# Layer 0 of a four-layer network: six of a Mamba item's 24 products with B formed with tokens on partitions by ScalarE and turned back by TensorE

## The chip, the core and the metric

The kernel is one program on one core of a Trainium2 chip. The metric is the device time in microseconds of the whole program, which computes four layers; only layer 0 is touched. The engines are TensorE (PE in the profile; its weight loads are PEld), VectorE (DVE), ScalarE (ACT), GpSimd (POOL) and SyncE (SP), which here issues every DMA. Each engine carries out its own instructions in the order in which they were put in its queue. SBUF is the on-chip memory, PSUM the small one into which TensorE writes.

## The reference

Layer 0 is two Mamba blocks one after the other, then a mix with a pooled branch and a batch normalisation. Cut to what matters:

```python
B, C, H, W = (4, 96, 64, 64)            # L = 4096 tokens
NLAYERS, DSTATE, EXPAND, DCONV = (2, 16, 2, 4)   # DIN = 192
...
    xz = h @ in_w
    xs, z = jnp.split(xz, 2, axis=-1)
    ...
    xc = jax.nn.silu(xc)
    dbl = xc @ xproj_w
    dt = dbl[..., :DTRANK]
    Bm = dbl[..., DTRANK:DTRANK + DSTATE]
    Cm = dbl[..., DTRANK + DSTATE:]
    delta = jax.nn.softplus(dt @ dt_w + dt_b)
    A = -jnp.exp(A_log)
    dA = jnp.exp(delta[..., None] * A)
    dBx = delta[..., None] * Bm[:, :, None, :] * xc[..., None]
    ...
    hstates = jax.lax.associative_scan(comb, (dA, dBx), axis=1)[1]
    y = jnp.einsum('blds,bls->bld', hstates, Cm) + Dp * xc
    y = y * jax.nn.silu(z)
    return y @ out_w
```

So for each of 192 channels and 16 states, along 4096 tokens: a factor `dA`, a term `dBx` (delta times xc times B), a running sum of the two, and a product with C that is summed over the states.

## The kernel before

**Items and tiles.** The work is cut into 32 items: 4 chunks of 1024 tokens, 2 blocks, 4 batch elements (`items`). An item has 192 x 16 = 3072 recurrences, which are 24 tiles of 128 partitions by 1024 tokens (`order`). A tile (p, g, j) has 4 states (group g of four) by 32 channels (half j of third p). A tile needs four steps:

- `exp` (ACT, line 464): dA = exp(A x delta). `ddb`, delta with each channel repeated for four states, comes by DMA from a copy in DRAM.
- the product of `udb` (delta times xc, repeated in the same way) with B. For eight tiles of an item, `pool_tiles`, POOL does it (`times_b`, line 470, output `up`) with `brep`, B repeated over 32 channels, which comes by DMA. For the other 16, PE repeats B into the PSUM tile `rep` (`rep`, line 450) and DVE multiplies (line 482).
- `scan` (DVE, line 486): the recurrence, output `hs`.
- `times_c` (POOL, line 492): `hs` times `crep`, C repeated.

PE then adds up the states of `hs` (`sum_y`, line 511) into `y`, to which `start_y` has put Dp x xc. Three times an item DVE multiplies `y` with silu(z) (`gate`), then `project` and `finish` form the block's output.

**First stage.** `first_stage(k)` makes what item k needs, spread over the two items before it: the normalisation (`center`, `nt`, `n`), `xc` (16 matmuls for each of three parts, line 210), its Silu, `dbl` (dt, B and C), `delta` with its Softplus, `z` with its Silu, `du` = delta x xc (three parts on POOL, line 378), and the DMAs that write `dd`, `ud` and `cd` to DRAM and load them repeated. Each step has a slot, `at_slot(t)`: it is put in the queues at tile t of the item before. Silu and Softplus need another table of ScalarE than Exp; `exp_set()` loads the Exp table back after each.

**Order.** The order is written out by hand: the loop over m at the end of the layer goes through all 768 tiles, and each pass issues the scan of tile m, then `rep` or `exp` of tile m + 1, `exp` of tile m + 3 (unless that is a POOL tile), `times_c` of m - 1, `keep_state` of m - 3, `times_b` as `b_slots` says, `sum_y`, `gate`, `project` and `finish`, and last the first-stage steps of that slot. POOL's and DVE's instructions, as all others, stand in this order.

**PSUM.** Its eight banks are full: two for `ps` (first stage and projection), two for `x` (one tile `rep`), two for `u` (one tile: the products `u` and, for POOL tiles, the exps `dap`), two for `y`.

```python
            eight = [(0, 0), (0, 1), (3, 0), (1, 1), (1, 0), (3, 1), (2, 0), (2, 1)]
            order = [(p, g, j) for p in range(3) for g, j in eight]
            pool_tiles = (2, 5, 7, 10, 13, 15, 18, 21)
            group_starts = (0, 3, 6, 8, 11, 14, 16, 19, 22)
```

Of the kernel before, what the change touches and what calls it, by code (L numbers as in the profile page):

```python
# [50 lines left out]
class Net:  # L51
# [43 lines left out]
    def layer0(self, dram, scratch):  # L95
        tc, nc, ins = self.tc, self.nc, self.ins
        x_in = ins["x"]
        with ExitStack() as ctx:
# [3 lines left out]
            psum_y = ctx.enter_context(tc.tile_pool(name="l0y", bufs=2, space=PSUM))  # L102
# [23 lines left out]
            sel_b = load(cp, "sel_b", [64, 4, 128])  # L126
# [24 lines left out]
            AHEAD = 3  # L151

# [48 lines left out]


            both = [(at, slice(64 * q, 64 * q + 64)) for q, at in enumerate(halves)]

            def spread(ws, rhs, p):

                ps = tile_ps(128)
                for k, (w, shift) in enumerate(ws):
                    for at, rows in both:
                        nc.tensor.matmul(  # L210
                            ps[rows],
                            w[:, 64 * p : 64 * p + 64],
                            rhs[:, at.start + shift : at.stop + shift],
                            start=k == 0,
                            stop=k == len(ws) - 1,
                            skip_group_check=True,
                        )
                return ps
# [10 lines left out]
            def global_pool():  # L229

                for b in range(B):
                    for s in range(NSC):
                        xt = wk.tile([128, T + 1], F32, name="gp_x", tag="hs", bufs=9)[:C, :T]
# [21 lines left out]
            def first_stage(k):  # L255
# [29 lines left out]
                def _():  # L285
                    m["nt"] = cp.tile([128, 8, C], F32, name="nt", tag="nt")
# [51 lines left out]
                @at_slot(4)  # L338
                def _():
                    nc.scalar.activation(m["xc"], m["xc"], AF.Silu)  # L340
                    exp_set()

# [3 lines left out]
                @at_slot(7)  # L346
# [4 lines left out]
                @at_slot(8)  # L351
# [6 lines left out]
                parts_of("delta", [(dtw[:, i], 0)], dbl, ((9, 10), (9, 10), (10, 11)), 1)  # L358

                @at_slot(11)  # L360
# [4 lines left out]
                parts_of("z", [(w_z[:, i], 3)], n, ((11, 12), (12, 13), (13, 14)), 3)  # L365

                @at_slot(12)
# [5 lines left out]
                def du(p):  # L373
# [3 lines left out]
                    u = wk.tile([128, 1, MB], F32, name="du", tag="du")  # L377
                    nc.gpsimd.tensor_mul(u, m["delta"][:, of], m["xc"][:, of])  # L378
# [3 lines left out]

                for p in range(3):
                    at_slot(14 + 3 * p)(lambda p=p: du(p))

                @at_slot(16)
                def _():
                    nc.scalar.activation(m["z"], m["z"], AF.Silu)
                    exp_set()


# [4 lines left out]
                for g, t in ((0, 10), (1, 21), (3, 23), (2, 25)):  # L396
                    at_slot(t)(lambda g=g: load_c(m, g))
                at_slot(19)(lambda: load_b(m, 3))
                at_slot(15)(lambda: load_b(m, 2))
                return steps  # L400

# [9 lines left out]
            def load_c(made, g):  # L411
                made["crep", g] = load_s(made, "crep", NST + 4 * g, 5)

            def load_b(made, g):
                made["brep", g] = load_s(made, f"brep{g}", 4 * g, 1)
# [20 lines left out]
            def on_pool(m):  # L436
                return m % NTL in pool_tiles
# [16 lines left out]

            def exp(m):
# [10 lines left out]
            def times_b(m):  # L466
# [3 lines left out]
                nc.gpsimd.tensor_mul(u, made[k]["ud", h, j], made[k]["brep", g])  # L470

            def scan(m, x):
# [4 lines left out]
                if on_pool(m):  # L477
                    u = made[k].pop(("u", t))
                else:

                    u = x if on_pool(m + 1) else psum_x.tile([128, T], F32, name="u", tag="u")
                    nc.vector.tensor_mul(u, made[k]["ud", h, j], x)  # L482
                hs = made[k]["hs", t] = wk.tile([128, T + 1], F32, name="hs", tag="hs", bufs=9)
# [71 lines left out]
            b_slots = {2: 5, 4: 7, 7: 10, 9: 13, 12: 15, 15: 18, 18: 21, 23: NTL + 2}  # L555
# [3 lines left out]
            for m in sorted(stages[0])[:4]:  # L559
                for f in stages[0].pop(m):  # L560
                    f()
            prepare()
            wk = ctx.enter_context(tc.tile_pool(name="l0w", bufs=1))
            with tc.manual_schedule(engines=engines):
                gp = global_pool()
                first = min(stages[0])
                for m in range(first, last + 19):
# [3 lines left out]
                    if 0 <= m + 1 < last:  # L571
                        if on_pool(m + 1):
                            exp(m + 1)
                        elif (t + 1) % NTL in group_starts:
# [7 lines left out]
                    if -1 <= m and t in b_slots and m - t + b_slots[t] < last:  # L582
# [767 lines left out]
def _constants():  # L1350
# [3 lines left out]
    sel_b = np.stack([(k[:64, None] % 32 == 4 * g + p[None] // 32) for g in range(4)], 1)  # L1354
# [127 lines left out]
```

## Time and profile before

| | |
|---|---|
| median of three runs | 3918.07 us (3902.56 to 3920.63) |
| the profiled execution | 3925.66 us, its span 3923.9 us |
| granted TensorE clock, mean over the span | 0.855 |
| first and last scan of layer 0 | start at 77.3 us, end at 2612.5 us |
| DMA | 463.31 MB, 46.7% of 16 engines |

The span is what the profile covers, from the first instruction to the last. In the page, a group of instructions gives the line, the engine, the operation, output<-inputs by the program's names, the shapes and the count; after the bar stand the busy time of all and the mean in nanoseconds of one, then the idle time of the engine just before them and what ended most of it. In a timeline the columns are start, duration, engine, line, operation, tiles, count, and in brackets the idle time before and what ended it. In an answer on waits they are who waited for whom, the sum, how often and the longest. An engine's idle time counts only where others wait for that engine.

### The profile page before, as it was taken

The numbers are of one execution on the slowest core, as the hardware profiler recorded it, in microseconds if no ns is written. First come the engines' busy times: TensorE is split into PE (matmuls) and PEld (weight loads), VectorE is DVE, ScalarE is ACT, GpSimd is POOL, SyncE is SP. The second block draws the span as 40 slices with busy tenths as digits, with TensorE's granted clock in tenths as the row PEclk, the third lists the DMA queues.
The fourth block names the chain that finished last, engine by engine and source line by source line (L and its number), as shares of the span: only waits on it lengthen the run. The fifth ranks groups of instructions, "written<-read, shape, count | busy, mean of one in ns | idle before, by whom it ended". The sixth has DMA issues, their size and how long they took to land. (4 is left out here: it accounts for less than half of the span.)

```text
span 3923.9 us, 43975 instructions
## 1 busy us (share of the span) xinstructions
PE 3205.9 (82%) x13534; PEld 1294.8 (33%) x13534; DVE 3154.4 (80%) x2772; ACT 2420.6 (62%) x4644; POOL 2911.4 (74%) x1443
## 2 busy tenths in 40 slices
PE   6887878877878788877878887755899988899988
PEld 3222222222222222222222222115644534666643
DVE  5999999999999999999999999973374385444649
ACT  4666667766766676666766666532254676666557
POOL 2999999999999999999999999961101064444427
PEclk7788878898788888888878878766899999999989
DMA  7567656675666566756676566636300000011101
GB/s 188 135 162 171 151 130 168 164 170 131 164 158 173 132 165 154 172 140 158 153 171 150 143 161 163 159 90 211 140 1 0 1 1 6 15 36 33 39 7 59
DMA packets 179828, 463.31 MB, mean 118 GB/s; under 512 B 52852, under 2 KB 54782, under 8 KB 176256
## 3 DMA queue, kind: packets, MB, share of 16 engines
q1 hardware_dynamic: 179592, 460.49, 46.7%
q8 instruction: 108, 1.77, 0.2%
q14 instruction: 128, 1.05, 0.1%
HBM read 386.81 MB, written 73.50 MB: 117 GB/s over the span
## 5 line engine op out<-in xcount | busy, mean ns | idle before, releaser
L492 POOL TENSOR_TENSOR hs<-hs,crep 128x1024 f32<-128x1024 f32 x768 | 1797.7, 2364 | 48.0 <-DVE hs L486 26.1
L450 PE MATMUL rep<-dbl,sel_b 32*128 32x512 f32 x1152 | 407.8, 785 | 495.8 <-DVE hs L486 428.3
L464 ACT ACTIVATE da<-ddb,nega 128x1024 f32<-128x1024 f32 x512 | 584.9, 1150 | 47.2 <-DVE hs L486 40.0
L470 POOL TENSOR_TENSOR up<-udb,brep 128x1024 f32<-128x1024 f32 x256 | 605.2, 2364 | 8.8 <-DMA brep<-cd 8.8
L464 ACT ACTIVATE dap<-ddb,nega 128x1024 f32<-128x1024 f32 x256 | 286.0, 1117 | 409.3 <-DVE hs L486 408.5
L511 PE MATMUL y<-hs,sel_r 128*32 128x512 f32 x3072 | 476.4, 690 | 5.5 <-POOL hs L492 5.5
L486 DVE TENSOR_TENSOR_SCAN hs<-da,state,rep 128x1024 f32<-128x1024 f32 x192 | 450.8, 2348 | 16.7
L486 DVE TENSOR_TENSOR_SCAN hs<-da,state,u 128x1024 f32<-128x1024 f32 x192 | 450.9, 2348 | 11.2 <-DVE u L482 1.4
L486 DVE TENSOR_TENSOR_SCAN hs<-dap,state,up 128x1024 f32<-128x1024 f32 x192 | 446.7, 2326 | 0.4 <-ACT dap L464 0.4
L210 PE MATMUL ps<-n,w_x 97*64 97x512 f32 x1536 | 408.0, 679 | 9.3 <-ACT n L319 6.6
L482 DVE TENSOR_TENSOR u<-udb,rep 128x1024 f32<-128x1024 f32 x256 | 314.7, 1229 | 74.4 <-PE rep L450 46.0
L450 PEld LDWEIGHTS rep<-dbl,sel_b 32*128 32x128 f32 x1152 | 107.0, 214 | 794.5 <-issue 595.7
L482 DVE TENSOR_TENSOR rep<-udb,rep 128x1024 f32<-128x1024 f32 x256 | 310.3, 1212 | 0.2
L1040 POOL CAST hq<-y 128x1536 fp8e5<-128x1536 f16 x64 | 94.0, 1469 | 219.3 <-issue 122.6
L210 PEld LDWEIGHTS ps<-n,w_x 97*64 97x64 f32 x1536 | 118.6, 153 | 295.2 <-issue 243.5
L511 PEld LDWEIGHTS y<-hs,sel_r 128*32 128x32 f32 x3072 | 65.2, 114 | 336.5 <-issue 208.5
L378 POOL TENSOR_TENSOR du<-delta,xc 128x512 f32<-128x512 f32 x96 | 122.6, 1277 | 64.7 <-ACT delta L362 50.2
L914 POOL MEMSET h<- 1x4096 f32 x1 | 3.5, 3507 | 212.8 <-DVE n L820 212.8
L1179 POOL TENSOR_TENSOR av<-av,ec 128x780 f32<-128x780 f32 x32 | 58.8, 1837 | 133.2 <-ACT av L1176 133.2
L486 DVE TENSOR_TENSOR_SCAN hs<-da,rep 128x1024 f32<-128x1024 f32 x64 | 146.5, 2289 | 5.4
L224 PE MATMUL ps<-xc,xproj 64*102 64x512 f32 x384 | 147.3, 924 | 3.5 <-ACT xc L340 3.5
L486 DVE TENSOR_TENSOR_SCAN hs<-da,u 128x1024 f32<-128x1024 f32 x64 | 146.4, 2288 | 3.7 <-DVE u L482 0.5
(262 smaller groups left out, 6137.7 us busy)
## 6 DMA issues: line engine op xcount, KB each, us to landing
ddb<-dd SPq DMA_DIRECT2D x768, 128.0 KB
udb<-ud SPq DMA_DIRECT2D x768, 128.0 KB
crep<-cd SPq DMA_DIRECT2D x512, 128.0 KB
brep<-cd SPq DMA_DIRECT2D x256, 128.0 KB
dd<-delta SPq DMA_DIRECT2D x64, 384.0 KB
ud<-du SPq DMA_DIRECT2D x192, 128.0 KB
band<-in_band SPq DMA_DIRECT2D x24, 1024.0 KB
x<-in_x SPq DMA_DIRECT2D x32, 384.0 KB
```

The source lines that it names most:

```text
L210: nc.tensor.matmul(ps[rows], w[:, 64 * p : 64 * p + 64], rhs[:, at.start + shift : at.stop + shift], start=k == 0, stop=k == len(ws) - 1, ...
L224: nc.tensor.matmul(ps, w[rows, p], x[rows, p], start=start and p == 0, stop=p == 2)
L378: nc.gpsimd.tensor_mul(u, m["delta"][:, of], m["xc"][:, of])
L450: nc.tensor.matmul(x[:, at], sel_b[rows, order[t][1]], made[k]["dbl"][rows, at], start=True, stop=True)
L464: nc.scalar.activation(da, made[k]["dd", h, j], AF.Exp, scale=nega[:, col : col + 1])
L470: nc.gpsimd.tensor_mul(u, made[k]["ud", h, j], made[k]["brep", g])
L482: nc.vector.tensor_mul(u, made[k]["ud", h, j], x)
L486: nc.vector.tensor_tensor_scan(hs[:, 1:], made[k].pop(("da", t)), u, 0.0 if s == 0 else st, ALU.mult, ALU.add)
L492: nc.gpsimd.tensor_mul(hs[:, :T], hs[:, 1:], made[k]["crep", order[t][1]])
L511: nc.tensor.matmul(made[k]["y", p][row : row + 32], sel_r, made[k]["hs", t][:, at], start=False, stop=True, skip_group_check=True,)
L1040: nc.gpsimd.tensor_copy(q, y2, saturate=False)
L1179: nc.gpsimd.tensor_add(v[:, 2:4], v[:, 0:2], ec)
```

## The change

An item's 24 products with B are split differently: 12 on DVE (groups g = 0 and 1), 6 on POOL (`GP` = 3), and 6 (`GA` = 2) with tokens on partitions. For these, PE turns `du` (`turn_du`: 12 transposes of 128 x 128) and B (8 small ones) so that tokens lie on partitions, ACT copies them out (`keep_du`, `bt`) and multiplies (`weigh`: 32 instructions of 192 elements each, B as the scalar of each partition), and PE turns the results back (`turn_u`: 8 transposes of 128 x 128 a tile) into the PSUM tile `x`, from which the scan reads.

With it: the order of the tiles is new (in p = 0 four tiles of DVE, then turned, POOL, turned, POOL; the others alike), `b_slots` with it; `du` of p = 1 goes to DVE; the first stage's slots move; the Silu of `z` stands beside that of the next item's `xc`; `y` has one PSUM buffer in place of two, and the freed bank takes the new turns and `z` (`turn_ps`); `hs` has 8 buffers in place of 9, `nt` lies in the buffers of `up`, `crep` has one buffer for each of four names in place of five in rotation, and B is loaded for one group in place of two; every product of DVE writes `u`, where before half of them were written over `rep`; `sum_y`, `gate`, `project` and `finish` move by one to four slots.

```diff
-            psum_y = ctx.enter_context(tc.tile_pool(name="l0y", bufs=2, space=PSUM))
+            psum_y = ctx.enter_context(tc.tile_pool(name="l0y", bufs=1, space=PSUM))
...
+            def turn_ps():
+                return psum_y.tile([128, MB], F32, name="t_ps", tag="t")
...
-                    m["nt"] = cp.tile([128, 8, C], F32, name="nt", tag="nt")
+                    if k:
+                        nt = wk.tile([128, T], F32, name="nt", tag="up", bufs=2)
+                    else:
+                        nt = first_pool.tile([128, T], F32, name="nt")
+                    m["nt"] = nt[:, : 8 * C].rearrange("p (q c) -> p q c", q=8)
...
                     nc.scalar.activation(m["xc"], m["xc"], AF.Silu)
+                    if k:
+                        silu_z(k - 1)
                     exp_set()
+
+                if k == len(items) - 1:
+                    at_slot(28)(lambda: (silu_z(k), exp_set()))
 
                 nb = 6 * NST + DTR
                 dbl = m["dbl"] = dbls[k % 2]
 
-                @at_slot(7)
+                @at_slot(6)
                 def _():
                     m["ps"] = [tile_ps(128), tile_ps(128)]
                     join([ps[:nb] for ps in m["ps"]], xproj[:, :, i], m["xc"])
 
-                @at_slot(8)
+                @at_slot(7)
                 def _():
                     for at, ps in zip(halves, m["ps"]):
                         nc.scalar.copy(dbl[:nb, at], ps[:nb])
                     cd = m["cd"] = dram.tile([2 * NST, T], F32, name="cd", tag="cd", bufs=2)
                     nc.sync.dma_start(cd, dbl[: 2 * NST])
 
-                parts_of("delta", [(dtw[:, i], 0)], dbl, ((9, 10), (9, 10), (10, 11)), 1)
-
-                @at_slot(11)
+                @at_slot(8)
+                def _():
+                    m["tb"] = turn_ps()[:, : 8 * 2 * NST].rearrange("p (q s) -> p q s", q=8)
+                    for q in range(8):
+                        nc.tensor.transpose(
+                            m["tb"][:, q], dbl[: 2 * NST, q * 128 : q * 128 + 128], self.ident[: 2 * NST, : 2 * NST]
+                        )
+
+                parts_of("delta", [(dtw[:, i], 0)], dbl, ((8, 9), (8, 9), (9, 10)), 1)
+
+                @at_slot(9)
+                def _():
+                    m["bt"] = cp.tile([128, 8, 4], F32, name="bt", tag="bt")
+                    nc.scalar.copy(m["bt"], m["tb"][:, :, 4 * GA : 4 * GA + 4])
+
+                @at_slot(10)
                 def _():
                     nc.scalar.activation(m["delta"], m["delta"], AF.Softplus)
                     exp_set()
 
-                parts_of("z", [(w_z[:, i], 3)], n, ((11, 12), (12, 13), (13, 14)), 3)
-
-                @at_slot(12)
+                @at_slot(11)
...
-                    u = wk.tile([128, 1, MB], F32, name="du", tag="du")
-                    nc.gpsimd.tensor_mul(u, m["delta"][:, of], m["xc"][:, of])
+                    u = m["du"] = wk.tile([128, 1, MB], F32, name="du", tag="du")
+                    (nc.vector if p == 1 else nc.gpsimd).tensor_mul(u, m["delta"][:, of], m["xc"][:, of])
                     to = m["ud"].rearrange("(p c) t -> c p t", p=3)[:, of]
                     for at, rows in both:
                         nc.sync.dma_start(to[:, :, at], u[rows])
 
+                def turn_du(p):
+                    ps = m["ut", p] = turn_ps() if p == 0 else tile_ps(128)
+                    for q in range(4):
+                        at = slice(q * 128, q * 128 + 128)
+                        nc.tensor.transpose(ps[:, at], m["du"][:, 0, at], self.ident)
+
+                def keep_du(p):
+                    if p == 0:
+                        udt = wk.tile([128, 3, MB], F32, name="udt", tag="delta", bufs=1)
+                        m["udt"] = udt.rearrange("p a b -> p (a b)").rearrange("p (q d) -> p q d", q=8)
+                    nc.scalar.copy(
+                        m["udt"][:, :, 64 * p : 64 * p + 64].rearrange("t (h q) d -> t q h d", h=2),
+                        m.pop(("ut", p)).rearrange("t (q h d) -> t q h d", q=4, h=2),
+                    )
+
                 for p in range(3):
-                    at_slot(14 + 3 * p)(lambda p=p: du(p))
-
-                @at_slot(16)
-                def _():
-                    nc.scalar.activation(m["z"], m["z"], AF.Silu)
-                    exp_set()
-
+                    at_slot(12 + 2 * p)(lambda p=p: turn_du(p))
+                    at_slot(11 + 2 * p)(lambda p=p: du(p))
+                    at_slot((16, 16, 17)[p])(lambda p=p: keep_du(p))
+
+                def weigh(of):
+                    if of[0] == 0:
+                        m["uta"] = wk.tile([128, 8, 6, 128], F32, name="uta", tag="uta", bufs=1)
+                    for e in of:
+                        q, s4 = divmod(e, 4)
+                        nc.scalar.mul(
+                            m["uta"][:, q, :, 32 * s4 : 32 * s4 + 32],
+                            m["udt"][:, q].rearrange("t (c d) -> t c d", d=32),
+                            m["bt"][:, q, s4 : s4 + 1],
+                        )
+
+                for e in range(9):
+                    at_slot(18 + e)(lambda e=e: weigh(range(32 * e // 9, 32 * (e + 1) // 9)))
+
+                def into_z(p):
+                    if p == 0:
+                        m["z"] = wk.tile([128, 3, MB], F32, name="z", tag="z", bufs=2)
+                    nc.scalar.copy(m["z"][:, p], m.pop(("z", p)))
+
+                for p in range(3):
+                    at_slot(20 + p)(lambda p=p: into_z(p))
+                    at_slot(19 + p)(lambda p=p: m.update({("z", p): spread([(w_z[:, i], 3)], n, p, turn_ps())}))
...
-                for g, t in ((0, 10), (1, 21), (3, 23), (2, 25)):
-                    at_slot(t)(lambda g=g: load_c(m, g))
-                at_slot(19)(lambda: load_b(m, 3))
-                at_slot(15)(lambda: load_b(m, 2))
+                for g, t in ((0, 22), (1, 23), (GA, 25), (GP, 27)):
+                    at_slot(t)(lambda g=g: load_c(m, g, k))
+                at_slot(17)(lambda: load_b(m))
                 return steps
+
+            def silu_z(k):
+                nc.scalar.activation(made[k]["z"], made[k]["z"], AF.Silu)
...
-                made["crep", g] = load_s(made, "crep", NST + 4 * g, 5)
-
-            def load_b(made, g):
-                made["brep", g] = load_s(made, f"brep{g}", 4 * g, 1)
+            def load_c(made, g, k):
+                made["crep", g] = load_s(made, f"crep{(g + 2 * k) % 4}", NST + 4 * g, 1)
+
+            def load_b(made):
+                made["brep"] = load_s(made, "brep", 4 * GP, 1)
...
-            eight = [(0, 0), (0, 1), (3, 0), (1, 1), (1, 0), (3, 1), (2, 0), (2, 1)]
-            order = [(p, g, j) for p in range(3) for g, j in eight]
-            pool_tiles = (2, 5, 7, 10, 13, 15, 18, 21)
-            group_starts = (0, 3, 6, 8, 11, 14, 16, 19, 22)
+            dd, ap = [(g, j) for g in range(2) for j in range(2)], [(GA, 0), (GP, 1), (GA, 1), (GP, 0)]
+            order = [(p, g, j) for p, gs in enumerate((dd + ap, dd[:2] + ap + dd[2:], ap + dd)) for g, j in gs]
...
+            def turned(m):
+                return order[m % NTL][1] == GA
...
+            def turn_u(m):
+
+                k, t = divmod(m, NTL)
+                p, g, j = order[t]
+                x = psum_x.tile([128, T], F32, name="ua", tag="x")
+                for q in range(8):
+                    nc.tensor.transpose(x[:, q * 128 : q * 128 + 128], made[k]["uta"][:, q, 2 * p + j], self.ident)
...
+                elif turned(m):
+                    u = x
                 else:
 
-                    u = x if on_pool(m + 1) else psum_x.tile([128, T], F32, name="u", tag="u")
+                    u = psum_x.tile([128, T], F32, name="u", tag="u")
                     nc.vector.tensor_mul(u, made[k]["ud", h, j], x)
-                hs = made[k]["hs", t] = wk.tile([128, T + 1], F32, name="hs", tag="hs", bufs=9)
+                hs = made[k]["hs", t] = wk.tile([128, T + 1], F32, name="hs", tag="hs", bufs=8)
...
-            b_slots = {2: 5, 4: 7, 7: 10, 9: 13, 12: 15, 15: 18, 18: 21, 23: NTL + 2}
+            b_slots = {8: 11, 9: 13, 14: 17, 15: 19, 21: NTL + 5, 1: 7}
...
+                        elif turned(m + 1):
+                            x = turn_u(m + 1)
+                        elif order[(t + 1) % NTL][2] == 0:
                             x = rep(m + 1)
...
-                            if at == 8 * p + 3:
+                            if at == 8 * p + 5:
                                 start_y(k0, p)
 
-                            if at - 8 * p in (4, 6, 8, 10):
-                                sum_y(k0, at - 4)
-                            if at == 8 * p + 11:
+                            if at - 8 * p in (5, 7, 9, 11):
+                                sum_y(k0, at - 5)
+                            if at == 8 * p + 12:
                                 gate(k0, p)
-                        if at == 34:
+                        if at == 31:
                             made[k0]["x"] = load_x(*items[k0])
-                        if at == 39:
+                        if at == 35:
                             project(k0)
-                        if at == 41:
+                        if at == 37:
```

More of the change, by code (lines that the diff above doesn't have):

```diff
@@ L125, in layer0 @@
             sel_r = load(cp, "sel_r", [128, 32])
-            sel_b = load(cp, "sel_b", [64, 4, 128])
+            sel_b = load(cp, "sel_b", [64, 2, 128])
             xproj = load(cp, "xproj", [128, 3, 2, 3 * 2 * NST + DTR])
@@ L151, in layer0 @@
             AHEAD = 3
+            GA, GP = 2, 3
             def prepare():
@@ L200, in tile_ps, with spread @@
                 return psum.tile([128, MB], F32, name="ps", tag="ps")[:rows]
+            def turn_ps():
+                return psum_y.tile([128, MB], F32, name="t_ps", tag="t")
             both = [(at, slice(64 * q, 64 * q + 64)) for q, at in enumerate(halves)]
-            def spread(ws, rhs, p):
-                ps = tile_ps(128)
+            def spread(ws, rhs, p, ps=None):
+                if ps is None:
+                    ps = tile_ps(128)
                 for k, (w, shift) in enumerate(ws):
@@ L232, in global_pool @@
                     for s in range(NSC):
-                        xt = wk.tile([128, T + 1], F32, name="gp_x", tag="hs", bufs=9)[:C, :T]
+                        xt = wk.tile([128, T + 1], F32, name="gp_x", tag="hs", bufs=8)[:C, :T]
                         nc.sync.dma_start(xt, x_in[b, :, s * T : (s + 1) * T])
@@ L409, in load_s @@
                 return t
-            def load_c(made, g):
-                made["crep", g] = load_s(made, "crep", NST + 4 * g, 5)
-            def load_b(made, g):
-                made["brep", g] = load_s(made, f"brep{g}", 4 * g, 1)
+            def load_c(made, g, k):
+                made["crep", g] = load_s(made, f"crep{(g + 2 * k) % 4}", NST + 4 * g, 1)
+            def load_b(made):
+                made["brep"] = load_s(made, "brep", 4 * GP, 1)
             def load_d(made, k, p, j):
@@ L436, in on_pool @@
             def on_pool(m):
-                return m % NTL in pool_tiles
+                return order[m % NTL][1] == GP
+            def turned(m):
+                return order[m % NTL][1] == GA
             def column(t):
@@ L452, in rep @@
                     )
+                return x
+            def turn_u(m):
[4 more added lines that the diff above has]
+                    nc.tensor.transpose(x[:, q * 128 : q * 128 + 128], made[k]["uta"][:, q, 2 * p + j], self.ident)
                 return x
@@ L469, in times_b @@
                 u = made[k]["u", t] = wk.tile([128, T], F32, name="up", tag="up", bufs=2)
-                nc.gpsimd.tensor_mul(u, made[k]["ud", h, j], made[k]["brep", g])
+                nc.gpsimd.tensor_mul(u, made[k]["ud", h, j], made[k]["brep"])
             def scan(m, x):
@@ L552, in finish @@
                 nc.sync.dma_start(scratch[:, a : a + T] if i else xd[:, b], o)
-            b_slots = {2: 5, 4: 7, 7: 10, 9: 13, 12: 15, 15: 18, 18: 21, 23: NTL + 2}
+            b_slots = {8: 11, 9: 13, 14: 17, 15: 19, 21: NTL + 5, 1: 7}
             engines = {mybir.EngineType.PE, mybir.EngineType.DVE, mybir.EngineType.Activation, mybir.EngineType.Pool}
             stages = [first_stage(k) for k in range(len(items))]
[L559 to L562, printed above, removed]
+            with tc.tile_pool(name="l0n", bufs=1) as first_pool:
+                for m in sorted(stages[0])[:4]:
+                    for f in stages[0].pop(m):
+                        f()
+                prepare()
             wk = ctx.enter_context(tc.tile_pool(name="l0w", bufs=1))
@@ L573, in layer0 @@
                             exp(m + 1)
-                        elif (t + 1) % NTL in group_starts:
+                        elif turned(m + 1):
+                            x = turn_u(m + 1)
+                        elif order[(t + 1) % NTL][2] == 0:
                             x = rep(m + 1)
@@ L581, in layer0 @@
                         keep_state(m - 3)
-                    if -1 <= m and t in b_slots and m - t + b_slots[t] < last:
+                    if -3 <= m and t in b_slots and m - t + b_slots[t] < last:
                         times_b(m - t + b_slots[t])
@@ L1352, in _constants @@
     p, k = np.arange(128), np.arange(C)
-    sel_b = np.stack([(k[:64, None] % 32 == 4 * g + p[None] // 32) for g in range(4)], 1)
+    sel_b = np.stack([(k[:64, None] % 32 == 4 * g + p[None] // 32) for g in range(2)], 1)
     sel_r = (p[:, None] % 32 == p[None, :32]).astype(f32)
```

## The prediction, made before the change was run

> **What bounds the kernel now.** I read the page's busy rows first, then the windows by stretch, the costliest groups, the waits of VectorE (DVE), and last the timelines of each engine over one item (one batch element, chunk and Mamba layer: 24 tiles).
>
> ```profile
> PE 3205.9 (82%) x13534; PEld 1294.8 (33%) x13534; DVE 3154.4 (80%) x2772; ACT 2420.6 (62%) x4644; POOL 2911.4 (74%) x1443
> ```
> ```profile
> 1000.00:1500.00 500.00, 403.52 (x1650) 116.76 (x1646) 477.96 (x271) 336.76 (x672) 489.76 (x222) 0.81 0.63 158
> ```
> The first is the whole span; the second is 500 us inside layer 0, with PE, PEld, DVE, ACT and POOL in that order. There, POOL is 98% busy, DVE 96%, PE 81%, ACT 67%. Two engines are full at once, so relieving one alone would give nothing.
>
> ```profile
> L492 POOL TENSOR_TENSOR hs<-hs,crep 128x1024 f32<-128x1024 f32 x768 | 1797.7, 2364 | 48.0 <-DVE hs L486 26.1
> L470 POOL TENSOR_TENSOR up<-udb,brep 128x1024 f32<-128x1024 f32 x256 | 605.2, 2364 | 8.8 <-DMA brep<-cd 8.8
> L486 DVE TENSOR_TENSOR_SCAN hs<-da,state,u 128x1024 f32<-128x1024 f32 x192 | 450.9, 2348 | 11.2 <-DVE u L482 1.4
> L482 DVE TENSOR_TENSOR u<-udb,rep 128x1024 f32<-128x1024 f32 x256 | 314.7, 1229 | 74.4 <-PE rep L450 46.0
> L482 DVE TENSOR_TENSOR rep<-udb,rep 128x1024 f32<-128x1024 f32 x256 | 310.3, 1212 | 0.2
> ```
> 32 items make 768 = 32 x 24 products with C, 256 = 32 x 8 products with B on POOL and 512 = 32 x 16 on DVE. The scans run from 75.6 to 2612.5 us: 79.3 us an item.
>
> ```profile
> DVE u L482 <- PE rep L450: 36.1, 32, 2.7
> ...
> DVE hs L486 <- ACT dap L464: 0.9, 2, 0.6
> ```
> These are DVE's waits from 300 to 2300 us, 25.2 items: about 1.4 us an item for `rep`, and next to nothing for ScalarE (ACT). Where the `rep` wait comes from:
>
> ```profile
> 1022.51 2.07 PE L450 MATMUL rep<-dbl,sel_b 32*128 32x512 f32 x4 [1.41 <-DVE u L482]
> 1024.52 5.67 PE L210 MATMUL ps<-n,w_x 97*64 97x512 f32 x16
> 1030.11 1.07 PE L511 MATMUL y<-hs,sel_r 128*32 128x512 f32 x8
> 1031.11 3.65 PE L210 MATMUL ps<-n,w_x 97*64 97x512 f32 x16
> 1034.69 1.13 PE L450 MATMUL rep<-dbl,sel_b 32*128 32x512 f32 x4
> ```
> ```profile
> 1032.08 2.32 DVE L486 TENSOR_TENSOR_SCAN hs<-dap,state,up 128x1024 f32<-128x1024 f32 x1
> 1035.87 1.23 DVE L482 TENSOR_TENSOR u<-udb,rep 128x1024 f32<-128x1024 f32 x1 [1.46 <-PE rep L450]
> ```
> TensorE (PE) runs in order, so the `rep` of the third tile stands behind two groups of 16 matmuls for the next item. The same work takes 1.13 or 2.07 us: after idle time it starts at half the clock. The other place to watch is ACT's Silu:
>
> ```profile
> 1040.65 0.58 ACT L329 COPY xc<-ps 128x512 f32<-128x512 f32 x1
> 1041.25 1.28 ACT L340 ACT_TABLE_LOAD   x1
> 1042.54 1.48 ACT L340 ACTIVATE xc<-xc 128x1536 f32<-128x1536 f32 x1
> 1044.04 1.28 ACT L227 ACT_TABLE_LOAD   x1
> 1045.34 1.15 ACT L464 ACTIVATE da<-ddb,nega 128x1024 f32<-128x1024 f32 x1
> 1046.39 0.17 ACT L499 COPY state<-hs 128x1 f32<-128x1 f32 x1
> 1046.47 1.11 ACT L464 ACTIVATE dap<-ddb,nega 128x1024 f32<-128x1024 f32 x1
> ```
> This `dap` is wanted by a scan that starts at 1049.31, so it has 1.7 us to spare.
>
> **The skill.** "SBUF — State Buffer", section Who interferes with whom: a DVE instruction with two SBUF inputs and a GpSimd instruction that reads SBUF lock each other out for a whole instruction. In the kernel before every product and scan has one input in PSUM, which fits both engines being 96 to 98% busy at once; the new `du` on DVE has two SBUF inputs, and no such pair is in the trace. "TensorE: Matmul & The Clock Gate", HAM oscillation: an idle gap above about 3.4 us puts the array back to half clock; agreed, gaps of 3.5 and 4.2 us are followed by a `rep` of 2.07 to 2.08 us. "ScalarE: Activation LUTs", What ACT_TABLE_LOAD costs: 1283 ns a load; the trace has 1283.
>
> **The change, part by part** (per item; `c` is a product with C, `up` one with B on POOL, A a turned tile, P a POOL tile, D a DVE tile).
>
> *DVE's own work.* From the timeline, start to start: product to scan 1.30 us, scan to the next instruction 2.26, 0.14 more if the next product writes PSUM tile `u` that the scan just read, a gate 0.58. Before: 16 x 1.30 + 24 x 2.26 + 8 x 0.14 + 3 x 0.58 = 77.9, and with 1.4 of waits 79.3, as measured. After: 12 x 1.30 + 24 x 2.26 + 12 x 0.14 (every D now writes `u`) + 1.7 = 73.3. The moved `du` is 0.7 (as the 128x512 gate's 0.67); its wait for POOL's lock is between 0 and 2.4 (one POOL product), 1.2 taken. Sum 75.2.
>
> *POOL.* Back to back a product is 2.335 us (4.70 for two). Before 32 of them and 3 `du` of 1.25: 78.5. After 30 and 2, and 0.7 of lock: 73.3.
>
> *ACT.* New: 32 `weigh` of 192 elements. From the `nt` multiplies (1.96 us for 8 of 96 elements) and the exps (1.05 for 1024) one is 0.33 us, 0.36 at most: 10.5 us. Three `keep_du` 1.7, one `bt` 0.3. Gone: two table loads, 2.6. ACT goes from 53 to 63 us of 79: room in total, but not everywhere.
>
> *PE.* Gone: three `rep` of 1.13 to 2.07. New: six `turn_u` of 8 transposes, 12 `du` transposes, 8 small ones. The 8 transposes of `nt` show the price:
> ```profile
> 1017.30 1.94 PE L308 MATMUL ps<-ident,nt 128*96 128x128 f32 x8
> ```
> and 1.08 us where the clock is full. With 128 columns in place of 96, 1.1 to 2.0 each. Net about 5 to 12 us, below PE's idle time. But `turn_u` writes the single PSUM tile `x`, so it can start only when the scan or product before has read it, and has one scan, 2.26 us, to finish: it fits if PE is free.
>
> *Queues and buffers.* SP loses four broadcasts of `brep` an item; the third `du` write now precedes the loads of `dd` (slot 16), which are wanted some 14 us later. `hs` with 8 buffers, one `y`, `nt` in `up`'s buffers: each is released several tiles before its next writer. I cost these at nothing.
>
> *New waits of DVE.* Set zero at the end of the scan of tile 3.
> (1) Tile 7. Exp 5 waits for that end because its `dap` takes `u` (done at 1.1), then state and `xc` copies, one load, both Silus (the second, `silu_z`, is new here), a load, exp 8, exp 7: 1.1 + 0.1 + 0.55 + 1.28 + 2 x 1.48 + 1.28 + 1.05 + 0.1 + 1.05 = 9.5. DVE, with three short tiles and a gate, wants it at 3 x 2.26 + 0.58 = 7.4. Wait 2.1. Behind the late exp 7 queue exps 9 and 10, which are not yet needed.
> (2) Tile 2. PE has `sum_y`, `w_x` 0, `w_x` 1 before its `rep`, as now less one `sum_y` (1.06); DVE arrives after D, D (7.4) in place of D, D, P (9.5). That makes 1.4 into 2.4. Besides, `udt` lies in `delta`'s buffer, so the first `keep_du` on ACT waits for the third `du`, and ACT, which has no gap from there to `w_x`'s input `n` (6 exps, 18 `weigh`, normalisation, `z`: 21 us), gives it later by about 0.6. Taken 3.0, between 1.5 and 5.0 (half clock).
> (3) Tile 18. The turn of the third `du` is queued on PE ahead of `turn_u` of 18, and that `du` on POOL comes after `up` of 11, 13, 17 and 19. From the end of scan 7, POOL must do 12 products and two `du` and give up 0.7: 12 x 2.335 + 2.5 + 0.7 = 31.2; then PE 0.6 + 1.1 + 0.1: 33.0, or 34.4 at half clock. DVE alone needs for that stretch four D of 3.70, six short tiles, gate, `du`: 29.7, and 0.6 where exp 13 stands behind Softplus and its two loads (0 to 2.7). So POOL's chain, not DVE, sets this stretch: 33.0, the lock's wait within it.
> The rest, tiles 18 to 7: 4.5 + 8 x 3.70 + 9.0 + two gates 1.2 = 44.3, and waits 3.0 + 2.1: 49.4.
>
> **Sum:** 33.0 + 49.4 = 82.4 us an item against 79.3: 3.1 x 32 = 99 us. The prologue gains `weigh` and turns, the tail loses little: nothing taken, 10 us either way kept. The profiled execution took 3925.66 us around a span of 3923.9: 4025; it was 7.6 above the median of 3918.07, so about 4017.
>
> **Rivals.** *The loads decide (faster).* The four exps in flight and eight `hs` buffers absorb the new waits, as they hide almost every one now (ACT cost DVE 0.9 us in 2000); only the old 1.4 stays, the item takes 75.2 + 1.4 = 76.6, and the time is 3918 - 2.7 x 32 = 3832. Place: tiles 2, 7 and 18; it decides if new waits and lock add less than 2.7 us an item over the 1.4. For it: both full engines lose 2.7 to 5 us of work. Against: `dap` can't run ahead, its tile `u` is single, as is `x`. *A draw:* waits eat the saving exactly, 3918. *PE at half clock (slower still).* Waiting on single buffers leaves gaps, turns take 2.0 of a window of 2.26, (2) costs 5.0 and (3) 34.4, and each of six turns slips by 0.3: 82.4 + 2.0 + 1.4 + 1.8 = 87.6, 4184 us. For it: cold `rep`s in the trace. Against: PE gets more work, so fewer long gaps.
>
> **How the numbers follow.** Forecast 0.56, the loads 0.25, a draw 0.09, half clock 0.10. A measurement can tell about 0.5% from no change. Slower 0.66, same 0.09, faster 0.25. The forecast's own range is 3945 to 4105 (waits (1) 1.6 to 2.6, (2) 1.5 to 5.0, (3) 32.3 to 34.4, `weigh` up to 0.36). The range reaches down to 3840, leaving out about half of the faster case, and up to 4105, leaving out the half-clock one.
>
> **What would show it.** Right: DVE's scans wait for ACT `dap` some 2 us an item and for PE `ua` at one tile in 24; POOL falls well below 98% and waits for DVE; `du` on DVE shows idle time or a duration above 0.7. Wrong: DVE above 97% busy in layer 0 with no wait over 1 us (then 76 us an item), `weigh` well off 0.33 us, or POOL still full (then its lock or its instructions grew).

## The result, and the profile after

The changed kernel takes 4170.47 us (median of four runs, 4169.73 to 4171.87) against 3919.35 us for the kernel before: 1.0649 times as long, 95% interval 1.0616 to 1.0681. That is 251 us more. The forecast had the direction, but 4017 us, with a range that ended at 4105.

The page of the changed kernel, beginning with its engines:

```profile
PE 3290.8 (79%) x15326; PEld 1484.9 (36%) x15326; DVE 3147.4 (76%) x2676; ACT 2728.6 (65%) x5734; POOL 2737.8 (66%) x1347
```

and the same 500 us inside layer 0 as before, columns PE, PEld, DVE, ACT, POOL, then clock and DMA:

```profile
1000.00:1500.00 500.00, 389.85 (x1820) 142.17 (x1818) 432.81 (x230) 358.37 (x796) 414.00 (x183) 0.81 0.56 138
```

No engine is full any more: POOL fell from 98 to 83%, DVE from 96 to 87%, and the latter still counts a `du` that mostly stands still. A longer time with less work on both full engines means waits. The scans of layer 0 run from 86.2 to 2862.5 us. Counted from the first product, which stands just ahead of the first scan, that is 86.8 us an item in place of 79.3; 7.5 x 32 is 240 of the 244.5 us by which the span grew. The first scan comes 9 us later, and what follows layer 0 is 5 us shorter.

DVE's waits over all of layer 0 (who for whom, sum, times, longest). The line left out is a single wait of 19.8 us for a DMA ahead of the first product:

```profile
DVE u L555 <- PE rep L512: 130.9, 80, 3.5
DVE z L595 <- PE y L584: 79.1, 31, 4.0
DVE hs L559 <- ACT dap L535: 73.8, 34, 3.0
...
DVE hs L559 <- PE ua L523: 13.4, 15, 1.6
```

Divided by 32: 4.1 us an item for `rep` (1.4 before), 2.5 for the gate, which did not wait before, 2.3 for `dap`, 0.4 for the turned tiles. One more loss is in no list of waits, since it is counted as busy time. It is in the page's groups:

```profile
L403 DVE TENSOR_TENSOR du<-delta,xc 128x512 f32<-128x512 f32 x32 | 139.6, 4361 | 9.2 <-DMA ud<-du 8.7
```

The one `du` that moved to DVE takes 4.36 us on average. A product of that size with one input in PSUM, the gate, takes 0.67. Added to the 73.3 us of other work that the prediction estimates: 73.3 + 4.4 + 4.1 + 2.5 + 2.3 + 0.4 = 87.0, against 86.8 measured.

The slow `du` in the timelines of DVE and of POOL (start, duration, engine, line, operation, tiles, count, idle time before):

```profile
1007.49 5.76 DVE L403 TENSOR_TENSOR du<-delta,xc 128x512 f32<-128x512 f32 x1
```
```profile
1003.41 6.99 POOL L565 TENSOR_TENSOR hs<-hs,crep 128x1024 f32<-128x1024 f32 x3
1010.37 2.33 POOL L541 TENSOR_TENSOR up<-udb,brep 128x1024 f32<-128x1024 f32 x1
1016.92 2.35 POOL L565 TENSOR_TENSOR hs<-hs,crep 128x1024 f32<-128x1024 f32 x1 [4.22 <-DVE hs L559]
```

POOL's queue passes two instruction ends, near 1008.07 and 1010.37, without letting `du` in. It runs dry at 1012.70, because its next product needs a scan that stands behind `du`, and `du` ends 0.55 us later. Then POOL idles for 4.22 us until that scan is done: both engines lose.

### The profile page after: what moved, and what is told of

Read it like the earlier page. It is cut to its first block, busy times and chain, and to the rows that moved or that the text cites. A ratio compares the mean times of both kernels' runs of the same rounds, so it can differ in the third digit from the quotient of the medians.

```text
span 4168.4 us, 48213 instructions
## 1 busy us (share of the span) xinstructions
PE 3290.8 (79%) x15326; PEld 1484.9 (36%) x15326; DVE 3147.4 (76%) x2676; ACT 2728.6 (65%) x5734; POOL 2737.8 (66%) x1347
## 5 line engine op out<-in xcount | busy, mean ns | idle before, releaser
L559 DVE TENSOR_TENSOR_SCAN hs<-da,state,u 128x1024 f32<-128x1024 f32 x288 | 676.3, 2348 | 30.6 <-DVE u L555 1.4
L555 DVE TENSOR_TENSOR u<-udb,rep 128x1024 f32<-128x1024 f32 x384 | 471.3, 1227 | 164.6 <-PE rep L512 130.9
L523 PE MATMUL ua<-ident,uta 128*128 128x128 f32 x1536 | 270.6, 334 | 295.9 <-DVE u L555 195.2
L541 POOL TENSOR_TENSOR up<-udb,brep 128x1024 f32<-128x1024 f32 x192 | 451.6, 2352 | 25.4 <-DMA udb<-ud 21.7
L433 ACT ACTIVATE uta<-udt,bt 128x192 f32<-128x192 f32 x1024 | 386.9, 455 | 0.0
L523 PEld LDWEIGHTS ua<-ident,uta 128*128 128x128 f32 x1536 | 220.2, 173 | 434.5 <-issue 218.5
L559 DVE TENSOR_TENSOR_SCAN hs<-da,state,ua 128x1024 f32<-128x1024 f32 x144 | 334.9, 2325 | 9.2 <-PE ua L523 9.2
L215 PE MATMUL t_ps<-n,w_z 97*64 97x512 f32 x384 | 149.5, 869 | 150.8 <-ACT z L445 150.8
L512 PE MATMUL rep<-dbl,sel_b 32*128 32x512 f32 x768 | 251.3, 734 | 15.2 <-DVE u L555 11.0
L403 DVE TENSOR_TENSOR du<-delta,xc 128x512 f32<-128x512 f32 x32 | 139.6, 4361 | 9.2 <-DMA ud<-du 8.7
```

Source lines behind the costliest of these rows:

```text
L215: nc.tensor.matmul(ps[rows], w[:, 64 * p : 64 * p + 64], rhs[:, at.start + shift : at.stop + shift], start=k == 0, stop=k == len(ws) - 1, ...
L403: (nc.vector if p == 1 else nc.gpsimd).tensor_mul(u, m["delta"][:, of], m["xc"][:, of])
L433: nc.scalar.mul(m["uta"][:, q, :, 32 * s4 : 32 * s4 + 32], m["udt"][:, q].rearrange("t (c d) -> t c d", d=32), m["bt"][:, q, s4 : s4 + 1],)
L512: nc.tensor.matmul(x[:, at], sel_b[rows, order[t][1]], made[k]["dbl"][rows, at], start=True, stop=True)
L523: nc.tensor.transpose(x[:, q * 128 : q * 128 + 128], made[k]["uta"][:, q, 2 * p + j], self.ident)
L541: nc.gpsimd.tensor_mul(u, made[k]["ud", h, j], made[k]["brep"])
```

## The experiments

Every time stands beside runs of the kernel before on the same chip: single ones of 3920 and 3922 us for the first eight experiments, medians of 3914 and 3918 us for the last four. The kernel before spread from 3898 to 3925 us over all its runs, so a difference of some ten microseconds between single runs says nothing. Waits are from 300 to 2500 us, 25 to 27 items by the length of an item in that run, unless said otherwise.

**The second du back on GpSimd.**

```diff
-                    (nc.vector if p == 1 else nc.gpsimd).tensor_mul(u, m["delta"][:, of], m["xc"][:, of])
+                    nc.gpsimd.tensor_mul(u, m["delta"][:, of], m["xc"][:, of])
```

> The second du of an item goes back from VectorE to GpSimd; nothing else differs from the changed kernel. Theory (the lock: VectorE with two SBUF inputs is held until GpSimd runs dry): the 4.36 us that du takes on VectorE fall away, GpSimd has 1.25 us more in its slack: about 3.5 us an item, 110 us, so about 4060 us. Rival (du is late because of its data: delta, or its single buffer, still being read): GpSimd's du waits for the same, the third du and the turns come as late as now, and the time stays within 30 us of 4170.

Measured: 4113.28 us, 57 less, so half of what the theory gave and not the rival's nothing. The other half went to a wait that was small before:

```profile
DVE u L555 <- PE rep L512: 104.0, 93, 3.5
DVE hs L559 <- PE ua L523: 86.1, 25, 4.2
DVE hs L559 <- ACT dap L535: 58.6, 26, 2.4
DVE z L595 <- PE y L584: 58.0, 26, 2.4
```

The second line is 3.3 us an item where the change as it stands had 0.4. It is wait (3) of the prediction, tile 18 behind the turn of the third `du`. PE's timeline in this run:

```profile
1343.38 1.11 PE L412 MATMUL ps<-ident,du 128*128 128x128 f32 x4 [3.42 <-POOL du L403]
1344.29 1.92 PE L523 MATMUL ua<-ident,uta 128*128 128x128 f32 x8
```

PE waits 3.42 us for POOL, then both turns take the longer of their two times (1.92 us for eight, where others take 1.06). In the changed kernel the lock had made DVE so late that most of this wait was covered; in the items where `du` was short there, tile 18 did wait, 1.56 us at 1109.78. The two don't add; the later one counts.

**Project one tile later.**

```diff
-                        if at == 35:
+                        if at == 36:
                             project(k0)
-                        if at == 37:
+                        if at == 38:
                             finish(k0)
```

> Project and finish of the item before are queued one tile later (36 and 38), so that TensorE adds up y for the first gate before it projects. Theory (the gate's 2.4 us wait is project's matmuls ahead of sum_y): the gate's wait for y falls below 0.5 us an item and the time by 60 to 75 us, to about 4100. Rival (GpSimd's product with C is late and project only fills the time): the gate waits as before, and the time stays within 20 us of 4170. In between, part of the gain is lost again at du's lock, since GpSimd then has more left to do when du comes: 4120 to 4150.

Measured: 4172.76 us, no gain, though the mechanism is confirmed: the gate's wait for `y` is gone from the list. In the changed kernel the loop takes the older item first, so at tile 11 PE does `project` of the item before (16 matmuls, the last 12 in the first line) ahead of the `sum_y` (second line) that the first gate (third line) needs:

```profile
1000.63 2.82 PE L229 MATMUL ps<-z,out_w 64*96 64x512 f32 x12
1003.38 1.07 PE L584 MATMUL y<-hs,sel_r 128*32 128x512 f32 x8
```
```profile
1004.54 0.69 DVE L595 TENSOR_TENSOR z<-y,z 128x512 f32<-128x512 f32 x1 [2.23 <-PE y L584]
```

The 64.2 us of that wait were spent at once in two other places. Waits for `dap` rose by 42.4 us, from 56.5 to 98.9: the scan of tile 13, no longer held back by the gate, now waits for its exp, which stands behind the Softplus and its two table loads. And `du` rose to 5.49 us, since POOL now had more left to do when it came, another 31 us. The middle course of the expectation, 4120 to 4150, allowed for the lock, but not for the exp.

**The Silu of z apart.**

```diff
-                    if k:
-                        silu_z(k - 1)
                     exp_set()
+                if k:
+                    at_slot(3)(lambda: (silu_z(k - 1), exp_set()))
```

> The Silu of z is moved ahead of tile 3's end, where ScalarE idles for 6 us, at the price of two more table loads (2.6 us of ScalarE an item). Theory (the scan of tile 7 waits 2.3 us for its exp behind both Silus): that wait goes to below 0.8 us, and the time falls by 45 to 70 us, to about 4110. Rival (ScalarE is full on the whole, 86% by the count of the prediction): the two loads push everything behind, no gain, 4170 or more.

Measured: 4126.35 us, 44 less, just short of the theory's gain; the wait for `dap` fell from 56.5 to 22.4 us, and `du` took 4.88 us in place of 4.36, so the lock took part of it back. In the changed kernel ACT does this ahead of tile 7's exp, the last line but one, and DVE waits for that exp:

```profile
1067.12 1.49 ACT L349 ACTIVATE xc<-xc 128x1536 f32<-128x1536 f32 x1
1068.51 1.47 ACT L461 ACTIVATE z<-z 128x1536 f32<-128x1536 f32 x1
1069.98 1.28 ACT L232 ACT_TABLE_LOAD   x1
...
1072.41 1.11 ACT L535 ACTIVATE dap<-ddb,nega 128x1024 f32<-128x1024 f32 x1
1073.62 2.35 DVE L559 TENSOR_TENSOR_SCAN hs<-dap,state,up 128x1024 f32<-128x1024 f32 x1 [2.25 <-ACT dap L535]
```

The change had saved two table loads by putting both Silus together, but the second one then held up an exp that DVE needed. Apart, with two loads more, both cost less.

**The kernel before, with its second du on VectorE.**

```diff
-                    nc.gpsimd.tensor_mul(u, m["delta"][:, of], m["xc"][:, of])
+                    (nc.vector if p == 1 else nc.gpsimd).tensor_mul(u, m["delta"][:, of], m["xc"][:, of])
```

> The kernel before with its second du on VectorE, nothing else. Theory (held until GpSimd runs dry): du takes 3 to 7 us on VectorE, the time rises by 80 to 200 us over 3918. Rival (held for one product of GpSimd at most, as the prediction priced it): du takes 0.7 to 3.0, mean about 1.9, GpSimd saves 1.25 of its own, and the time rises by less than 60 us.

Measured: 4113.72 us, 194 more than the kernel before, 6.05 us an item from one instruction in 24 tiles. The page:

```profile
L378 DVE TENSOR_TENSOR du<-delta,xc 128x512 f32<-128x512 f32 x32 | 202.4, 6324 | 0.0
```

And one of them, beside POOL:

```profile
1076.07 6.83 DVE L378 TENSOR_TENSOR du<-delta,xc 128x512 f32<-128x512 f32 x1
```
```profile
1073.09 6.95 POOL L492 TENSOR_TENSOR hs<-hs,crep 128x1024 f32<-128x1024 f32 x3
1080.01 2.34 POOL L470 TENSOR_TENSOR up<-udb,brep 128x1024 f32<-128x1024 f32 x1
1085.30 2.33 POOL L492 TENSOR_TENSOR hs<-hs,crep 128x1024 f32<-128x1024 f32 x1 [2.96 <-DVE hs L486]
```

Again POOL's queue ends (1082.35) before `du` does (1082.90). The rival, one POOL product at most, is out: 6.32 us on average, up to 9.25. In 30 of the 32 items `du` outlasted the whole of POOL's queue in this way; the two short ones met a POOL that was idle or ending its last product.

**The second du on VectorE, with delta in PSUM.**

```diff
+                    if p == 1:
+                        dp1 = psum_x.tile([128, T], F32, name="d_u", tag="u")[:, :MB]
+                        nc.scalar.copy(dp1, m["delta"][:, p])
+                        nc.vector.tensor_mul(u[:, 0], dp1, m["xc"][:, p])
```

> The second du stays on VectorE, but ScalarE first copies its delta into a free half of the PSUM tile u, so that only one input of du lies in SBUF. Theory (the lock comes with two SBUF inputs): du takes 0.7 us at any load of GpSimd; VectorE waits for the copy instead, 1 to 2 us; the third du on GpSimd then holds tile 18 as it does with all du on GpSimd: 4070 to 4120. Rival (du on VectorE is slow for another reason, its output, its shape or its place): du stays at 4 to 6 us and the time at 4170 or above.

Measured: 4093.80 us, 77 less. The same product on the same engine in the same place, with one input moved:

```profile
L406 DVE TENSOR_TENSOR du<-d_u,xc 128x512 f32<-128x512 f32 x32 | 22.1, 691 | 61.7 <-ACT d_u L405 44.0 <-POOL hs L570 10.1 <-DMA ud<-du 7.6
```

0.69 us in place of 4.36, each time, and in 31 of the 32 items POOL was at work throughout. DVE now waits 1.9 us an item for the copy and its like, as the last part of the line shows. So the two SBUF inputs make the lock, not the engine, the shape or the place. The time is in the theory's range, but one part of the theory fails: tile 18 is not held by the third `du` as it is with all `du` on POOL, its wait is 13.2 us in the window in place of 86.1.

**The products for z one tile later.**

```diff
-                    at_slot(20 + p)(lambda p=p: into_z(p))
-                    at_slot(19 + p)(lambda p=p: m.update(...
+                    at_slot(21 + p)(lambda p=p: into_z(p))
+                    at_slot(20 + p)(lambda p=p: m.update(...
```

> The three products for z and their copies are queued one tile later, so that rep of tile 22 stands ahead of the second of them. Theory (tile 22 waits 2 to 3 us for rep, because TensorE stands at z's second product until ScalarE has emptied the one PSUM bank of the turns): that wait goes, VectorE's sum of waits for rep falls from 4.3 us an item to 2.5 or less, part of it comes back at tile 2 (the products for xc come later): 4090 to 4135. Rival (TensorE as a whole is short of time at its half clock): the wait moves to the next rep in full and the time stays within 20 us of 4170.

Measured: 4124.36 us, 46 less; waits for `rep` fell from 110.0 to 46.0 us, while `du` rose to 4.94 us. What they had stood behind is in PE's timeline of the changed kernel:

```profile
1036.33 1.97 PE L215 MATMUL t_ps<-n,w_z 97*64 97x512 f32 x4 [3.74 <-ACT z L445]
1038.23 2.08 PE L512 MATMUL rep<-dbl,sel_b 32*128 32x512 f32 x4
```

`z` has one PSUM bank for its three parts. Its second part waits for ACT to empty the bank of the first, in ACT's densest stretch (weights, normalisation and exps without a gap), and `rep` of tile 22 waits behind it on PE.

**All edits at once.** To the four that helped or were neutral (du in PSUM, project later, Silu apart, z later) come two: the second product for `xc` goes behind `rep` of tile 2 (slot 1 for 0), and the turn of the third `du` behind `turn_u` of tile 18 (slot 17 for 16).

> All queue edits at once: du with one input in PSUM, project one tile later, the Silu of z apart, the products for z one tile later, the second product for xc behind rep of tile 2, the turn of the third du behind turn_u of tile 18. Theory (the change costs only through these waits, and its work is what the prediction summed, 73 to 75 us an item): 76 to 79 us an item, so 3820 to 3920, level with the kernel before or up to 2.5% below it. Rival (one wait only gives way to the next, since three engines are full): 83 us an item or more, above 4040.

Measured: 3974.94 us, 196 less than the change and 53 above the kernel before. That is 81.0 us an item, between the two readings: most of the loss was in these queues, but new waits took part of the gain (2.9 us an item for `rep`, now mostly of tile 20, behind the normalisation's matmuls, and 2.5 for `dap`).

> The same edits, but the second du goes to GpSimd instead. Theory: no lock either, GpSimd at 74 us an item against VectorE's 73: within 40 us of the run with du in PSUM. Rival (GpSimd's chain up to the third du decides): 60 us or more above it.

Measured: 4038.08 us, 63 above the other, so the rival: with `du` on POOL, waits for `dap` and `ua` come to 162 us in the window in place of 79. With this order `du` is better on DVE, but not with both inputs in SBUF.

**Two more queue edits.** The normalisation's matmuls one slot later, behind `rep` of tile 20, and the exp of a tile that follows a POOL tile behind that tile's own exp.

> All queue edits, and two more for the waits that their run still showed: the products for the normalisation come one tile later, behind rep of tile 20 (VectorE waited 3 us an item there), and the exp of a tile that follows a GpSimd tile is queued behind that tile's own exp (2.7 us an item at tiles 7 and 13). Theory (only queue order made the change dear): 76 to 78 us an item, 3820 to 3890, faster than the kernel before by 1 to 2.5%. Rival (the next wait takes the place): 80 us or more, 3950 or above.

Measured: 3935.17 us (median of eight), 1.0057 times the kernel before (1.0038 to 1.0076). The theory had said 3820 to 3890, so it fails, and the rival's 3950 is not reached either; but this is 235 us below the change. The waits at tiles 20 and 7 are gone, and in their place the first tile of an item waits about 3 us for `rep` or the DMA ahead of its product; in these two lines, from 300 to 2300 us, most is of that tile:

```profile
DVE u L569 <- DMA crep<-cd: 41.2, 15, 3.9
DVE u L569 <- PE rep L526: 35.2, 13, 5.7
```

What causes it was not tried. And with the lock put back into this kernel:

> The same with the second du on VectorE reading both inputs from SBUF, as the change has it. Theory (held until GpSimd runs dry): with fewer waits of VectorE elsewhere GpSimd has more left to do at that point, du takes 4 to 7 us, and the time is 100 to 170 us above the run with du in PSUM. Rival (the lock was only long because VectorE was late for other reasons): du below 2.5 us and less than 50 us between the two.

Measured: 4088.23 us, 153 more, `du` at 5.42 us. So against `du` with one input in PSUM the lock costs 77 us in the change and 153 here, where fewer other waits cover it. Against `du` on POOL it costs 57 us in the change and 194 in the kernel before.

**GpSimd's product of tile 19 behind the third du, and two buffers for du.**

```diff
-            b_slots = {8: 11, 9: 13, 14: 17, 15: 19, 21: NTL + 5, 1: 7}
+            b_slots = {8: 11, 9: 13, 14: 17, 16: 19, 21: NTL + 5, 1: 7}
```

> All edits of the last run but one, and GpSimd's product up of tile 19 queued one tile later, so that the third du comes 2.3 us earlier (ScalarE waited 2.8 us an item for it, just ahead of its densest stretch). Theory (that wait pushes the products for z, and with them rep of the next item): 77.5 to 79 us an item, 3850 to 3910, level with or faster than the kernel before. Rival (ScalarE, busy for 83% of the time, is the limit itself): within 15 us of 3935.

> The same, with two buffers for du in place of one, paid for by 7 buffers of hs in place of 8. Theory (VectorE's du waits up to 2.7 us for the DMA that still reads the first du): another 0.5 to 1 us an item, 15 to 30 us below the other run of this call. Rival (7 buffers of hs hold VectorE's scans until TensorE has added them up): slower than the other run by 20 us or more.

Measured with one buffer: 3928.69 us (eight runs), 1.0034 times the kernel before (1.0020 to 1.0049). That is 6 us below the last run, not the theory's 25 or more but the rival's figure; whether ACT is the limit, as the rival has it, this doesn't show. With two buffers: 3912.82 us (twenty runs), 0.9997 times (0.9986 to 1.0008). The second buffer gave 16 us, the low end of what was expected, and with 7 buffers of `hs` no wait for one shows in DVE's list. So the new split of the products can be had at the time of the old one, and no version that was run beats the kernel before beyond its interval. In the last one, 1000 to 1500 us:

```profile
1000.00:1500.00 500.00, 416.65 (x1985) 153.26 (x1983) 454.33 (x252) 417.97 (x904) 456.45 (x203) 0.86 0.66 151
```

DVE and POOL are 91% busy, ACT and PE 84 and 83%; in the kernel before, DVE and POOL were nearly full, with ACT at 67 and PE at 81%. My reading, which no run isolates, is that four engines which hand tiles to each other through single buffers leave gaps on each. DVE's largest waits left, from 300 to 2300 us, are 36.7 us for `rep`, 36.7 put down to the DMA of C, and 33.0 for the copy of `delta`.

## Why the prediction was wrong

*Direction and frame.* Right: the change costs through DVE's waits, not through work. Both engines' loads fell and the time rose. DVE's own work, estimated at 73.3 us, closes the sum with the measured waits and the `du`, to 0.2 us.

*The step that failed* is the `du` on DVE: "its wait for POOL's lock is between 0 and 2.4 (one POOL product), 1.2 taken". It measured 3.7 (4.36 less 0.67), and 23 of 32 are 5.2 to 6.1 us long. I took the page of the Trainium skill ("SBUF — State Buffer", Who interferes with whom), which says that the engine that issues first holds the shared pair of ports for the whole instruction and the other is blocked, to mean one instruction of the other engine. In most items the trace shows a whole queue of them. The upper end was wrong too, so the range did not cover it.

The trace of the kernel before could have told this. The prediction's "no such pair is in the trace" is a wrong reading: in the last layer DVE has a `zz<-av` with both inputs in SBUF, 0.55 us at the median and up to 2.73. In that longest one it outlasts three instructions of GpSimd, passing two ends, and is done 0.42 us after the third:

```profile
3583.04 2.73 DVE L1191 SCALAR_TENSOR_TENSOR zz<-av 128x384 f32<-128x384 f32 x1 [0.27 <-ACT av L1186]
```
```profile
3582.26 1.27 POOL L1117 TENSOR_TENSOR h<-h,ln_rs 96x512 f32<-96x512 f32 x1 [1.46 <-ACT ln_rs L1116]
3583.49 1.86 POOL L1152 TENSOR_TENSOR f<-p,p 128x390 f32<-128x390 f32 x2
```

In the sum it was hidden besides: part (3) let POOL's chain set the stretch from the end of scan 7 to the start of scan 18, 33.0 us, with "the lock's wait within it". The trace of the changed kernel has 36.1 us for that stretch on average over the items, and 50.7 for the rest, where 49.4 was forecast: 3.1 of the missing 4.4 us are here. The chain itself was nearly right: 33.8 us in an item with a short `du` (1075.97 to 1109.78). But with the lock DVE is later than the chain. Its 29.7 us of the prediction, with 2.5 of wait at the first gate, 3.7 at the lock and 0.4 at tile 18, make 36.3. With the 1.2 that was taken for the lock the same sum, without a wait at tile 18, is 33.4, an estimate: close to the chain, gate and all. So it is the size of the lock's wait that moved the stretch off the forecast.

*Two waits were not seen.* The first gate (2.5 us an item): the prediction does not price `project`, which moves from slot 39 to 35. The same tile 11 holds the `sum_y` for that gate, and the loop issues the older item's step first. What a moved step is put ahead of was not looked up for PE. And tile 22 behind `z`: of the 4.1 us of wait for `rep`, 2.4 are at tile 22, where nothing was forecast, and 1.3 at tile 2, where part (2) had 3.0 and where the wait stayed near the 1.4 of the kernel before. That 3.0 lies as near to 4.1 as it does is luck. The bank that takes the turns and `z` has no price in the prediction; of the other buffers it says that each is "released several tiles before its next writer". For `z` the next writer is one tile away, and ACT, which must empty the bank, is at its fullest there.

*What held.* Wait (1), tile 7: 2.25 us measured where 2.1 was forecast, by the sum of ACT's queue as written. Part (3)'s chain: tile 18 waits 0.4 us in the change, 3.3 with the second `du` back on POOL. The turns: 1.04 to 1.97 us, forecast 1.1 to 2.0. `weigh`: 0.35 us from one start to the next, forecast 0.33 and at most 0.36.

*The rivals.* The loads don't decide: both fell, and the item took 7.5 us longer. The rival at half clock named 4184 us, close to the result for another reason: the mean clock is 0.86 as before, and the turned tiles together cost DVE 0.4 us, not 1.8. The idle gap of 3.4 us that the prediction gives for the fall to half clock is no sharp line here: in the kernel before, a `rep` after 3.14 us of idle took 1.13 us at 1094.73, and 2.08 at 1176.02.

## What to carry to other kernels

A product moved to VectorE to relieve GpSimd was free of the lock here with one of its inputs in PSUM (0.69 us). With both in SBUF beside GpSimd's products, price its time as up to the rest of GpSimd's queue (4.36 to 6.32 us on average in these kernels, for 0.67 us of work), not as one instruction. Where several engines hand tiles over through single PSUM tiles, price a moved step by what stands behind it in its engine's queue at that very tile, other items' steps included. And a wait removed is worth only the distance to the next one in the same stretch: project alone gave nothing and `du` on GpSimd half, while together with the rest the edits gave over 200 us (235 to 258 in the last versions).

## What the hardware showed that I had not expected

The lock between VectorE and GpSimd is mostly not handed over at the end of an instruction. In the changed kernel 23 of the 32 `du` outlast every product that GpSimd has ready, across two instruction ends, and end 0.55 us after the last of them, when GpSimd has nothing left to do. But some get in between two products. In the run that put the lock back into the reordered kernel, 8 of the 32 `du` take 2.5 to 2.7 us, like this one:

```profile
211.00 2.54 DVE L409 TENSOR_TENSOR du<-delta,xc 128x512 f32<-128x512 f32 x1 [1.39 <-DMA ud<-du]
```
```profile
210.62 2.37 POOL L574 TENSOR_TENSOR hs<-hs,crep 128x1024 f32<-128x1024 f32 x1
212.94 2.81 POOL L550 TENSOR_TENSOR up<-udb,brep 128x1024 f32<-128x1024 f32 x1
```

Here `du` ends 0.55 us after the product that ran when it came, and it is GpSimd's next one that takes 2.81 us in place of 2.33: it stood still for about 0.5 us. In the changed kernel one item is of this kind (1.34 us), and three more `du` came within 0.15 us of the end of a product:

```profile
1095.81 0.69 DVE L403 TENSOR_TENSOR du<-delta,xc 128x512 f32<-128x512 f32 x1
```
```profile
1091.22 7.50 POOL L565 TENSOR_TENSOR hs<-hs,crep 128x1024 f32<-128x1024 f32 x3
```

This `du` takes 0.69 us in the middle of three products, which take 7.50 us together in place of 6.99. The other five short ones (0.67 to 0.69 us) found GpSimd idle or at the end of its last product. Timing alone doesn't settle who gets in: at 221.09 and at 305.68 `du` came equally long, 0.79 us, before the end of a product with another one behind it, and took 1.34 us the first time and 5.9 the second. Why is open. So the wait is anything from nothing to the rest of GpSimd's queue.
